# Two-layer masked attention on one core: putting the products with V off past large units of TensorE work

## The chip, the core and the metric

The kernel runs on one core of a Trainium2 chip. The metric is the device time of one execution in microseconds; the time before is the median of three runs.

## The reference

Two layers, each: layer norm with ReLU, masked multi-head attention with an adjacency mask, output projection, residual sum. There are 16 batches of 1024 rows with 256 features, all in float32. Layer 0 has 4 heads of 64 features, layer 1 has 8 heads of 32 and biases.

```python
# x (16, 1024, 256) float32, adj (16, 1024, 1024) int32, E = 256
def layer(x, adj, Wq, Wk, Wv, Wo, H, biases):
    h = maximum(layernorm(x), 0)
    q, k, v = heads(h, Wq), heads(h, Wk), heads(h, Wv)   # (16, H, 1024, E // H)
    s = einsum("bhnd,bhmd->bhnm", q, k) / sqrt(E // H)
    w = softmax(where(mask(adj), s, -inf), axis=-1)
    o = einsum("bhnm,bhmd->bhnd", w, v)
    return x + concat_heads(o) @ Wo.T + bo
x = layer(x, adj, ..., H=4)      # layer 0
x = layer(x, adj, ..., H=8)      # layer 1
```

## The kernel before

**Steps.** The attention is cut into *steps*. A step is four blocks of scores, each 128 keys by 512 queries, and everything that is done with them. Layer 0 of a batch has 16 steps (two heads and two key tiles each), layer 1 has 32 (four heads and one key tile each). The list of steps is fixed: layer 0 of batch 0, then, for each batch b, 16 steps of layer 0 of batch b+1 followed by 32 steps of layer 1 of batch b; the last batch leaves only the 32 of layer 1. In this document a+3 is the step with index 3 within such a block of 16, c+3 the step with index 3 within the block of 32 behind it. All blocks have an even number of steps, so a step's index is even or odd in the whole list as it is within its block. Groups of 4 (layer 0) or 8 (layer 1) steps share one accumulator `po`.

**What a step does.** `scores` (L364) multiplies K with Q on TensorE into two PSUM pairs `ps` (a pair is two banks; there are three pairs, L92, handed out in turn, and every other TensorE product except `po` and `pz` uses a pair of this same pool). `exponentials` has VectorE put the mask on each pair (L380, which frees the pair) and ScalarE take the exponential (L385), giving `p`. `weigh` (L396) multiplies `p` with V into `po`. `LEAD = 2`: step i of `Stream.run` issues the scores of step i and the products with V of step i-2.

**Column sums.** In layer 0 `add_tiles` adds blocks of `p` on VectorE and GpSimd (L407, L409). In layer 1 GpSimd adds the `p` of an odd step to that of the even step before it (L471), writing over the even one. `count` (L273) then multiplies with ones on TensorE into `pz`; it is entered in the list of things due two steps later. The tile `p` of even steps has three buffers, that of odd steps two.

**Units.** Between steps the other work of the stream is called from `self.due`, a table from step to calls that was filled by hand: `turn` (L195, transposes the normed rows), `k` and `q` (L207), `values` (L236) and, at the end of two groups, `end_half` (L345, output projection and residual). Each of `k`, `q`, `values` and `end_half` keeps TensorE busy for some 3.6 us; per batch there are 16 of them. Norm statistics (L160, L161), mask changes (L139), mask loads and transposes (L121, L125, L131) and the chain that inverts the sums (L288 to L316) hang on the same table.

**Shapes on TensorE.** Three kinds of product alternate, and the profile writes the part of the 128x128 array that each uses. Scores use row tiles, 64\*128 in layer 0 and 32\*128 in layer 1 (called R). `po` and `pz` use column tiles, 128\*64 and 128\*32 (called C). Units use the whole array, 128\*128 (called F). Order on each engine's queue is the order in which the program issues; no scheduler reorders.

**Start.** Before the stream the first batch's inputs and mask are made by straight code (L504 to L537): per tile of 128 rows, `load` (GpSimd's DMA queue), `flip` (a transposing DMA of SyncE's queue) and `put` (ScalarE, L131), with the first units among them.

Of the kernel before, what the change touches and what calls it, by code (L numbers as in the profile page):

```python
# [22 lines left out]
LEAD = 2  # L23
# [52 lines left out]
def fast_program(ctx, tc, a, w, loads, chk):  # L76
# [6 lines left out]
    NT = N // P  # L83
# [24 lines left out]
    def open_x(b, half):  # L108
        t = xp.tile([P, 4, E], F32, tag=f"x{half}", name=f"x_{b}_{half}")
        nc.sync.dma_start(t, x[b, ts(half, 512), :].rearrange("(t p) e -> p t e", p=P))  # L110
        xs[b, half] = t


    class Mask:
        def __init__(self, b):
            self.b, self.src, self.flipped = b, {}, {}
# [239 lines left out]
    def scores(st):  # L356
        gr = st.gr
        D = gr.D
        st.ps = [psum_pair(f"ps_{st.n}_{i}") for i in range(2)]
        st.blocks = []  # L360
        for i in range(4):
            r, kt = (i, st.j) if gr.layer else (i % 2, 2 * st.j + i // 2)
            st.blocks.append((r, kt))
            nc.tensor.matmul(  # L364
                st.ps[i // 2][:, i % 2, :],
                gr.inp.kT[r * D : (r + 1) * D, gr.g, ts(kt, P)],
                gr.inp.qT[r * D : (r + 1) * D, gr.g, ts(gr.qh, 512)],
                start=True, stop=True,
            )

    def exponentials(st, between):


        gr = st.gr
        odd = st.j % 2
        st.p = pp.tile([P, 4, 512], F32, tag=f"p{odd}", bufs=2 if odd else 3, name=f"p_{st.n}")
        for i in range(2):
            half = st.p[:, ts(i, 2), :]
            kt = st.blocks[2 * i][1]
            nc.vector.scalar_tensor_tensor(  # L380
                out=half,
                in0=gr.mask.m[:, kt, ts(gr.qh, 512)].unsqueeze(1).to_broadcast([P, 2, 512]),
                scalar=BIG, in1=st.ps[i], op0=ALU.mult, op1=ALU.min,
            )
            nc.scalar.activation(half, half, AF.Exp, scale=gr.scale)  # L385
            if i == 0:
                between()

    def weigh(st):
        gr = st.gr  # L390
        D = gr.D
        if st.j == 0:
            gr.o = ps_o.tile([P, 512], F32, tag="po", name=f"po_{gr.n}")
        for i, (r, kt) in enumerate(st.blocks):
            h = gr.g * gr.per + r
            nc.tensor.matmul(  # L396
                gr.o[r * D : (r + 1) * D, :], gr.inp.v[:, kt, h * D : (h + 1) * D],
                st.p[:, i, :], start=(kt == 0), stop=(kt == NT - 1),
            )

    def add_tiles(st):

        gr = st.gr
        t = work.tile([P, 2, 512], F32, tag="t", bufs=3, name=f"t_{st.n}")

        engine = nc.vector if st.j else nc.gpsimd
        engine.tensor_add(t, st.p[:, 0:2, :], st.p[:, 2:4, :])  # L407
        if st.j:
            nc.gpsimd.tensor_add(t, t, gr.t)  # L409
        gr.t = t  # L410

    def layer_steps(inp, mask):
        steps = []
        for qh in range(QH):
            half = Step()
            for g in range(2):
                steps += Group(inp, mask, qh, g, half).steps()
        return steps

    class Stream:  # L420

        def __init__(self, steps):
            self.steps, self.due = steps, {}

        def later(self, i, f, *args):
            self.due.setdefault(i, []).append((f, args))

        def run(self):  # L430
            steps = self.steps
            n = len(steps)
            for i in range(n + LEAD):
                now = steps[i] if i < n else None
                st = steps[i - LEAD] if i >= LEAD else None
                if now:
                    scores(now)
                copy = lambda: None
                if st:
                    weigh(st)  # L440
                    if st.gr.layer:
                        self.count_steps(i, st)
                    if st.last:
                        copy = st.gr.copy_out
                        self.end_group(i, st.gr)
                if now:
                    exponentials(now, copy)
                else:
                    copy()
                one = steps[i - 1] if 1 <= i <= n else None  # L450
                if one and one.gr.layer == 0:
                    add_tiles(one)
                for f, args in self.due.pop(i, []):
                    f(*args)
            while self.due:
                for f, args in self.due.pop(min(self.due)):
                    f(*args)
# [41 lines left out]
    def open_w(n):  # L499
        for _ in range(n):  # L500
            t, src = loads.pop(0)
            nc.sync.dma_start(t, src)

    masks = [Mask(b) for b in range(B)]  # L504
    inputs = [[Inputs(b, layer) for b in range(B)] for layer in range(2)]
    mask, inp = masks[0], inputs[0][0]
# [5 lines left out]
    inp.stats(0)  # L512
    inp.norm(0)
    inp.stats(1)
    inp.norm(1)
    for t in range(NT):
        mask.flip(t)
        mask.put(t)
        if t + 2 < NT:
            mask.load(t + 2)  # L520
        else:
            masks[1].load(t + 2 - NT)
        open_w(-(-len(loads) // 2))
        if t == 1:
            inp.turn(0)
            inp.k(0)
        if t == 3:
            inp.q(0)
            inp.turn(1)
        if t == 5:  # L530
            inp.values(0)
            inp.k(1)
    inp.q(1)
    inp.values(1)
    for half in range(QH):
        open_x(1, half)
        inp.add_bias(half)  # L537
# [14 lines left out]
    steps = layer_steps(inputs[0][0], masks[0])  # L552
# [11 lines left out]
    def norms(inp, half, i):  # L564

        later(i, inp.stats, half, (0, 1))
        later(i + 1, inp.stats, half, (2, 3))
        later(i + 3, inp.norm, half, (0, 1))
        later(i + 4, inp.norm, half, (2, 3))
        later(i + 5, inp.add_bias, half)  # L570

    def half_inputs(inp, half, *at):

        for i, f in zip(at, (inp.turn, inp.k, inp.q, inp.values)):
            later(i, f, half)
# [6 lines left out]
            later(2 * t + 1, masks[1].load, t + 2)  # L582
    for half in range(QH):
        norms(inputs[0][1], half, 3 * half)
    half_inputs(inputs[0][1], 0, 5, 6, 7, 8)
    half_inputs(inputs[0][1], 1, 9, 10, 11, 12)
    for b in range(B - 1):
        mine, a, c = inputs[1][b], first[b + 1], second[b]
        if b == 0:

            norms(mine, 0, a + 1)
            norms(mine, 1, a + 9)
            half_inputs(mine, 0, a + 6, a + 7, a + 8, a + 9)
            half_inputs(mine, 1, a + 15, c + 1, c + 4, c + 2)
        else:
            norms(mine, 0, a - 10)
            norms(mine, 1, a - 8)
            half_inputs(mine, 0, a - 4, a + 3, a + 4, a + 5)
            half_inputs(mine, 1, a - 2, a + 7, c + 4, c + 2)
        for kt in range(NT):  # L600
            later(a + 4 + kt, masks[b].second, kt)
        if b + 2 < B:
            other, mask = inputs[0][b + 2], masks[b + 2]
            later(a + 1, open_x, b + 2, 0)
            later(a + 11, open_x, b + 2, 1)
            norms(other, 0, a + 7)
            norms(other, 1, a + 15)
            half_inputs(other, 0, a + 14, c + 6, c + 10, c + 12)
            half_inputs(other, 1, c + 14, c + 16, c + 18, c + 20)
            for t in range(NT):  # L610
                i = a + 2 + 5 * t
                later(i, mask.load, t)
                later(i + 3, mask.flip, t)
                later(i + 5, mask.put, t)
        else:
            last = inputs[1][b + 1]
            norms(last, 0, c + 1)
            norms(last, 1, c + 9)
            half_inputs(last, 0, c + 6, c + 10, c + 12, c + 14)
            half_inputs(last, 1, c + 16, c + 20, c + 36, c + 34)  # L620
            for kt in range(NT):
                later(c + 8 + 2 * kt, masks[b + 1].second, kt)
# [162 lines left out]
def kernel(  # L785
# [28 lines left out]
    with ExitStack() as fast, tc.manual_schedule():  # L814
        fast_program(fast, tc, a, w, loads, chk)
# [61 lines left out]
```

## Time and profile before

| | |
|---|---|
| time, median of 3 runs | 3465.09 us (3464.63 to 3465.22) |
| profiled execution | 3465.88 us, its span 3464.0 us |
| granted TensorE clock | 0.997 |
| PE busy | 3402.7 us (98%), 18190 matmul rows |
| DVE busy | 2465.9 us (71%) |
| ACT busy | 2177.0 us (63%) |
| POOL busy | 2447.1 us (71%) |
| first scores on PE | 45.66 us |
| last matmul of the stream (L331) begins its group | 3446.98 us |

PE is TensorE, DVE VectorE, ACT ScalarE, POOL GpSimd, SP SyncE. A matmul of float32 is two rows of the profile. The end of a matmul row is modelled and overlaps with the next, so the busy share of PE says that it is seldom empty, not that it is streaming; the distance from the start of one group of rows to the start of the next is what a group really took.

### The profile page before, as it was taken

Reading aid. Unit: us, or ns where it says so; the run is one execution under the profiler, and the core shown is the slowest. Engines: PE = TensorE matmul, PEld = TensorE weight load, DVE = VectorE, ACT = ScalarE, POOL = GpSimd, SP = SyncE. Lnnn points to the kernel's source line nnn. Section 1 sums busy time; section 2 is a strip of 40 time slices with the busy share of each in tenths; the row PEclk is TensorE's granted clock in tenths of the full one; section 3 lists DMA queues with packets and bytes.
Section 4 is the critical chain, followed back from the end, with each engine's and each line's share of the span. In section 5 each row is a group of like instructions: output and inputs, shape, how many; then the busy total and the mean of one; then the engine's idle time right before and its main releaser. Section 6 shows DMA issues by size and latency. Waiting matters only on the chain. (4 is left out here: it accounts for less than half of the span.)

```text
span 3464.0 us, 46246 instructions
## 1 busy us (share of the span) xinstructions
PE 3402.7 (98%) x18190; PEld 1283.5 (37%) x18190; DVE 2465.9 (71%) x2664; ACT 2177.0 (63%) x2402; POOL 2447.1 (71%) x1606
## 2 busy tenths in 40 slices
PE   7999999999999999999999999999999999999998
PEld 3333333333333333333333433333333333333332
DVE  4777767777677676777767777677776776767776
ACT  5556566675666756667566675666756666665665
POOL 4677676776677766777667776677767777776766
PEclk9999999999999999999999999999999999999999
DMA  6121221211112121121211221212121121120000
GB/s 134 40 42 33 47 38 35 50 37 45 35 35 50 41 41 35 38 48 40 46 37 36 44 41 44 38 36 44 40 47 35 47 41 35 47 38 20 11 17 30
DMA packets 250738, 141.77 MB, mean 41 GB/s; under 512 B 182416, under 2 KB 217488, under 8 KB 250512
## 3 DMA queue, kind: packets, MB, share of 16 engines
q1 hardware_dynamic: 232080, 105.18, 12.6%
q0 software_dynamic: 18432, 33.56, 6.4%
q8 instruction: 144, 2.36, 0.3%
q14 instruction: 82, 0.67, 0.1%
HBM read 120.33 MB, written 18.34 MB: 40 GB/s over the span
## 5 line engine op out<-in xcount | busy, mean ns | idle before, releaser
L380 DVE SCALAR_TENSOR_TENSOR p<-mask,ps 128x1024 f32<-128x1024 fp8e4 x1536 | 1797.3, 1214 | 687.3 <-PE ps L364 682.5
L385 ACT ACTIVATE p<-p 128x1024 f32<-128x1024 f32 x1536 | 1613.4, 1056 | 1000.0 <-DVE p L380 959.2
L471 POOL TENSOR_TENSOR p<-p,p 128x2048 f32<-128x2048 f32 x255 | 1160.6, 4553 | 349.4 <-PE po L396 274.6
L364 PE MATMUL ps<-qT,kT 32*128 32x512 f32 (+1 forms) x6144 | 1172.0, 633 | 15.2 <-ACT hT L196 6.8
L396 PE MATMUL po<-p,v 128*32 128x512 f32 (+1 forms) x6144 | 1043.5, 606 | 14.8 <-ACT o L280 14.2
L409 POOL TENSOR_TENSOR t<-t,t 128x1024 f32<-128x1024 f32 x192 | 468.7, 2441 | 447.5 <-DVE t L407 415.6
L364 PEld LDWEIGHTS ps<-qT,kT 32*128 32x128 f32 (+1 forms) x6144 | 378.1, 184 | 722.3 <-issue 359.5
L396 PEld LDWEIGHTS po<-p,v 128*32 128x32 f32 (+1 forms) x6144 | 205.0, 117 | 749.5 <-issue 466.7
L407 DVE TENSOR_TENSOR t<-p 128x1024 f32<-128x1024 f32 x192 | 286.2, 1491 | 4.5 <-POOL t L409 4.5
L273 PE MATMUL pz<-p,ones 128*32 128x512 f32 x2056 | 267.7, 593 | 0.0
L207 PE MATMUL pq<-hT,wk 128*128 128x512 f32 x512 | 240.9, 614 | 8.1 <-ACT hT L196 8.1
L236 PE MATMUL pv<-wv,hT 128*128 128x256 f32 x1024 | 237.9, 385 | 0.0
L207 PE MATMUL pq<-hT,wq 128*128 128x512 f32 x512 | 236.6, 605 | 0.0
L345 PE MATMUL py<-wo,cat 128*128 128x256 f32 x1008 | 234.6, 386 | 0.5 <-POOL cat L316 0.5
L236 PEld LDWEIGHTS pv<-wv,hT 128*128 128x128 f32 x1024 | 189.4, 190 | 75.2 <-issue 28.9
L345 PEld LDWEIGHTS py<-wo,cat 128*128 128x128 f32 x1008 | 186.3, 190 | 75.3 <-issue 27.5
L316 POOL TENSOR_TENSOR cat<-o,inv 128x512 f32<-128x512 f32 x127 | 164.7, 1297 | 23.2 <-DMA inv<-vd 17.1
L407 POOL TENSOR_TENSOR t<-p 128x1024 f32<-128x1024 f32 x64 | 151.7, 2370 | 2.8 <-ACT p L385 2.4
L207 PEld LDWEIGHTS pq<-hT,wk 128*128 128x128 f32 x512 | 93.7, 193 | 154.9 <-issue 117.8
L131 ACT ACTIVATE mask<-adjT,mhalf 128x1024 fp8e4<-128x1024 bf16 x128 | 145.6, 1139 | 2.3 <-DMA adjT<-adj 2.1
L207 PEld LDWEIGHTS pq<-hT,wq 128*128 128x128 f32 x512 | 92.2, 189 | 144.3 <-issue 130.5
L177 ACT ACTIVATE hn<-x,shift,rstd 128x256 f32<-128x256 f32 x256 | 138.1, 587 | 11.0 <-POOL shift L170 11.0
(52 smaller groups left out, 1615.5 us busy)
## 6 DMA issues: line engine op xcount, KB each, us to landing
adj<-in_adj_dram POOLq DMA_DIRECT2D x128, 256.0 KB, 3.7
x<-in_x_dram SPq DMA_DIRECT2D x32, 512.0 KB
inv<-vd SPq DMA_DIRECT2D x128, 128.0 KB
inv<-vd SPq DMA_DIRECT2D x252, 64.0 KB
out_dram<-x SPq DMA_DIRECT2D x31, 512.0 KB
adjT<-adj SPq DMA_TRANSPOSE x128
sd<-s SPq DMA_DIRECT2D x64, 4.0 KB
sn<-sd SPq DMA_DIRECT2D x64, 4.0 KB
```

What stands on the lines that cost most here:

```text
L207: nc.tensor.matmul(pq[:, m, :], wt[self.layer][:, c, ts(m, P)], self.hT[half][:, c, :], start=(c == 0), stop=(c == 1),)
L236: nc.tensor.matmul(pv[:, i, :], self.hT[half][:, c, ts(i, P)], w.v[self.layer][:, c, :], start=(c == 0), stop=(c == 1),)
L273: nc.tensor.matmul(self.s[r * self.D : (r + 1) * self.D, :], w.ones[:, : self.D], p[:, r, :], start=start, stop=stop,)
L316: nc.gpsimd.tensor_mul(self.half.cat[:, self.g, :], self.ob, self.inv)
L345: nc.tensor.matmul(py[:, i, :], self.half.cat[:, c, ts(i, P)], w.o[self.layer][:, c, :], start=(c == 0), stop=(c == 1),)
L364: nc.tensor.matmul(st.ps[i // 2][:, i % 2, :], gr.inp.kT[r * D : (r + 1) * D, gr.g, ts(kt, P)], gr.inp.qT[r * D : (r + 1) * D, gr.g, ts(gr ...
L380: nc.vector.scalar_tensor_tensor(out=half, in0=gr.mask.m[:, kt, ts(gr.qh, 512)].unsqueeze(1).to_broadcast([P, 2, 512]), scalar=BIG, in1=st ...
L385: nc.scalar.activation(half, half, AF.Exp, scale=gr.scale)
L396: nc.tensor.matmul(gr.o[r * D : (r + 1) * D, :], gr.inp.v[:, kt, h * D : (h + 1) * D], st.p[:, i, :], start=(kt == 0), stop=(kt == NT - 1),)
L407: engine.tensor_add(t, st.p[:, 0:2, :], st.p[:, 2:4, :])
L409: nc.gpsimd.tensor_add(t, t, gr.t)
L471: nc.gpsimd.tensor_add(one, one, st.p)
```

## The change

`Stream.run` no longer calls `weigh` for step i-2 in every step i. Steps are put in a list `waiting`, and the list is emptied when i is odd or when nothing large (`k`, `q`, `values`, `end_half`) is due in step i. In an even step with something large due, `weigh` is left to step i+1, which calls it twice. What follows `weigh` (`count_steps`, `end_group`) is called with it. The table is altered so that large units stand at even steps: those called in layer 0's steps, and layer 0's own in the first 16. The inputs of the first batch are made in another order: the first `turn` goes ahead of the mask transposes, and the `put`s come later, in twos.

```diff
+        def large(self, i):
+            return any(
+                f.__name__ in ("k", "q", "values", "end_half") for f, _ in self.due.get(i, [])
+            )
@@ Stream.run
+            waiting = []
             for i in range(n + LEAD):
                 now = steps[i] if i < n else None
-                st = steps[i - LEAD] if i >= LEAD else None
+                if i >= LEAD:
+                    waiting.append(steps[i - LEAD])
                 if now:
                     scores(now)
                 copy = lambda: None
-                if st:
-                    weigh(st)
-                    if st.gr.layer:
-                        self.count_steps(i, st)
-                    if st.last:
-                        copy = st.gr.copy_out
-                        self.end_group(i, st.gr)
+                if i % 2 or not self.large(i):
+                    for st in waiting:
+                        weigh(st)
+                    for st in waiting:
+                        if st.gr.layer:
+                            self.count_steps(i, st)
+                        if st.last:
+                            copy = st.gr.copy_out
+                            self.end_group(i, st.gr)
+                    waiting = []
                 if now:
                     exponentials(now, copy)
@@ inputs of the first batch
     inp.stats(0)
     inp.norm(0)
     inp.stats(1)
-    inp.norm(1)
-    for t in range(NT):
-        mask.flip(t)
-        mask.put(t)
-        if t + 2 < NT:
-            mask.load(t + 2)
-        else:
-            masks[1].load(t + 2 - NT)
-        open_w(-(-len(loads) // 2))
-        if t == 1:
-            inp.turn(0)
-            inp.k(0)
-        if t == 3:
-            inp.q(0)
-            inp.turn(1)
-        if t == 5:
-            inp.values(0)
-            inp.k(1)
-    inp.q(1)
-    inp.values(1)
+    inp.turn(0)
+
+    def tiles(*ts):
+        for t in ts:
+            mask.flip(t)
+            (mask if t + 2 < NT else masks[1]).load((t + 2) % NT)
+            open_w(-(-len(loads) // 2))
+
+    tiles(0, 1)
+    inp.k(0)
+    inp.norm(1)
+    inp.q(0)
+    inp.turn(1)
+    mask.put(0)
+    mask.put(1)
+    inp.values(0)
+    tiles(2, 3)
+    inp.k(1)
+    mask.put(2)
+    mask.put(3)
+    tiles(4, 5)
+    inp.q(1)
+    mask.put(4)
+    mask.put(5)
+    tiles(6, 7)
+    inp.values(1)
+    mask.put(6)
+    mask.put(7)
@@ the table: half_inputs(inputs, half, turn, k, q, values)
-    half_inputs(inputs[0][1], 0, 5, 6, 7, 8)
-    half_inputs(inputs[0][1], 1, 9, 10, 11, 12)
+    half_inputs(inputs[0][1], 0, 5, 6, 8, 10)
+    half_inputs(inputs[0][1], 1, 11, 12, 14, 16)
@@ b == 0
-            half_inputs(mine, 0, a + 6, a + 7, a + 8, a + 9)
-            half_inputs(mine, 1, a + 15, c + 1, c + 4, c + 2)
+            half_inputs(mine, 0, a + 6, a + 8, a + 10, a + 12)
+            half_inputs(mine, 1, a + 15, c, c + 4, c + 2)
@@ b > 0
-            half_inputs(mine, 0, a - 4, a + 3, a + 4, a + 5)
-            half_inputs(mine, 1, a - 2, a + 7, c + 4, c + 2)
+            half_inputs(mine, 0, a - 4, a + 2, a + 4, a + 6)
+            half_inputs(mine, 1, a - 2, a + 8, c + 4, c + 2)
```

## The prediction

> **What bounds the kernel now.** I read the page's busy table first, then the table of who PE waited for, then PE's timeline.
>
> ```profile
> PE 3402.7 (98%) x18190; PEld 1283.5 (37%) x18190; DVE 2465.9 (71%) x2664; ACT 2177.0 (63%) x2402; POOL 2447.1 (71%) x1606
> PE po L396 <- ACT o L280: 14.2, 30, 0.7
> PE ps L364 <- DVE p L380: 6.3, 5, 2.6
> ```
>
> PE is the engine that sets the end: no other is over 71%, and its listed waits are few. But the ends of matmul rows are modelled, so real gaps hide inside the 98%. They show as distances between starts:
>
> ```profile
> 1290.19 1.14 PE L364 MATMUL ps<-qT,kT 32*128 32x512 f32 x8
> 1291.26 1.94 PE L396 MATMUL po<-p,v 128*64 128x512 f32 x8
> 1293.12 3.72 PE L345 MATMUL py<-wo,cat 128*128 128x256 f32 x16
> 1296.78 1.14 PE L364 MATMUL ps<-qT,kT 32*128 32x512 f32 x8
> 1297.85 1.94 PE L396 MATMUL po<-p,v 128*64 128x512 f32 x8
> 1299.71 1.79 PE L364 MATMUL ps<-qT,kT 32*128 32x512 f32 x8
> 1302.00 1.06 PE L396 MATMUL po<-p,v 128*32 128x512 f32 x8 [0.50 <-ACT o L280]
> ...
> 1307.65 1.14 PE L364 MATMUL ps<-qT,kT 32*128 32x512 f32 x8
> 1308.72 1.07 PE L396 MATMUL po<-p,v 128*32 128x512 f32 x8
> 1309.72 1.51 PE L364 MATMUL ps<-qT,kT 32*128 32x512 f32 x8
> 1311.16 1.06 PE L396 MATMUL po<-p,v 128*32 128x512 f32 x8
> 1312.16 3.70 PE L207 MATMUL pq<-hT,wq 128*128 128x512 f32 x8
> 1315.79 1.14 PE L364 MATMUL ps<-qT,kT 32*128 32x512 f32 x8
> 1316.86 1.07 PE L396 MATMUL po<-p,v 128*32 128x512 f32 x8
> 1317.74 1.04 PE L273 MATMUL pz<-p,ones 128*32 128x512 f32 x8
> 1318.71 1.14 PE L364 MATMUL ps<-qT,kT 32*128 32x512 f32 x8
> ```
>
> The second column is modelled, the first is when PE began. Within a group a new set of tiles starts each 0.427 us, so a layer-1 `po` streams 2 x 0.427 = 0.853 and a layer-0 `po` 1.707. Yet 1308.72 to 1309.72 is 0.996 and 1291.26 to 1293.12 is 1.868: each costs 0.143 or 0.161 more. Where `pz` follows `po` (both C), 1316.86 to 1317.74 is 0.883, and the 0.12 appears behind `pz`. Over all groups the medians are: R to C 0.21 over streaming, C to anything else 0.143 (32 columns) or 0.161 (64), F to R 0.22 to 0.24. So **a run of one kind costs some 0.11 at its end plus the first weight load at its start**.
>
> Beside this some steps are late: the scores at 1299.71 (step c+2) take 2.29 instead of 1.07. Summing such excess over the trace gives 121 us, nearly all in layer 1: c+2 16.1, c+4 5.6, c+23 to c+26 46.7, c+29 and c+31 22, c+15 6.7, c+10 and c+18 3.0.
>
> **What the Trainium skill says.** "TensorEngine Tiling", Key Properties: changing the tiling mode drains the engine. The trace agrees, with 0.11 where the kind changes and none between `po` and `pz`. "TensorE: Matmul & The Clock Gate", LDWEIGHTS: a load takes its columns over 1.2 ns, so 107, 53 and 27 ns for 128, 64 and 32 columns. With the 0.11 this gives 0.21, 0.16 and 0.14, the measured three. "SBUF — State Buffer", Who interferes with whom: VectorE in a two-port mode and GpSimd lock each other out. The trace has it: L139 takes 0.68 us, but 4.45 at 3290.10, ending as two GpSimd sums do. I use it below for the last batches only.
>
> **The change part by part.**
>
> 1. *Fewer runs.* Before, a large unit's surroundings are R C F R C; after, R F R CC. I counted runs in the instruction streams of both programs as built: 246 pairs of `po` now stand together (152 of layer 1, 94 of layer 0). Runs of C fall by 152 (32 columns) and by 78 (64 columns, since 16 `po` had been joined to a `pz` before), and two units now touch: 232 switches fewer of 1903. 152 x 0.143 + 78 x 0.161 + 2 x 0.22 = **34.7 us**, on PE's path. R to F does not occur in the trace before. I price it as R to C, 0.21, because the closing cost hardly depends on what follows. Without any drain it would save another 246 x 0.107 = 26; with a second load's worth on top it would cost 26.
>
> 2. *Steps c+0 to c+5.* At c+2 PE waits for a PSUM pair that VectorE has not read: VectorE is behind with statistics (1.08), the residual sum L350 (1.19) and sums (1.22). Moving `po` behind the next scores gives VectorE time. On the clock above, with VectorE's own durations: scores c+0 1290.19; L345 at 1291.26 to 1294.91; scores c+1 at 1294.91, their second pair held to 1295.9 as VectorE reads c+0 until 1295.80, so done by 1296.4; two `po` 1.76 + 1.82; scores c+2 1300.0 to 1301.07; then `values` needs the pair that VectorE frees at 1301.4, so 1301.5 to 1305.15; `pz`; scores c+3 at 1306.15, two `po`; c+4 at 1309.1, no wait; L207 1310.15; scores c+5 1313.8; c+6 at 1317.6 against 1318.71 before. That is 1.1 us a batch, 0.45 of it counted in 1: 15 x 0.65 = **9.8 us**. Two new waits (0.47 at c+1, 0.4 at c+2) eat half of what the old ones gave.
>
> 3. *Steps c+20 to c+27.* Here VectorE is the bound: exponentials' mask 2.35 plus statistics 1.1 in each step, from c+22 on. Scores of c+22 come 0.15 earlier, so VectorE's chain starts 0.17 earlier. At c+26 `po` also waited for ScalarE's copy of the last `po` (L280); it now goes to c+27, and L345 instead waits for the pair freed at about 1185.6 on that batch's clock (1187.29 before). Scores c+28 then come at 1193.1 against 1193.87: 0.8 a batch, 0.29 counted: 15 x 0.5 = **7.7 us**. At c+10 and c+18 the same copy is no longer waited for: **3.0 us**.
>
> 4. *Units moved to even steps* (k of a+3 to a+2, values a+5 to a+6, k a+7 to a+8, and in the first batches). No instruction is added; the copies to SBUF on ACT and DVE go along, and SP and POOL issue the same. Layer 0's steps have no PE waits before (2.6 us in all); for a pair of steps DVE has up to 10 us of work (masks 4.7, sums 2.4, q's copy 1.4, L139 1.4) in over 11 us of PE. Cost zero; a wait of 0.4 us in each of some 75 would be 30.
>
> 5. *GpSimd's sums L471* wait for the even step's `po`, which now comes a step later. In a pair with a unit that is 2.1 to 6.7 us after the pair's first scores, 4.55 more for the sum; `pz` reads it a pair (8.5 us) later. VectorE overwrites the odd `p` two steps later: margin 0.7 us at c+23, over 1 elsewhere. Cost zero.
>
> 6. *The start.* Now `turn` and `k` needn't wait for ScalarE's two `put`s (7.7 us on PE), but the last `put` still ends the chain: transposes wait for buffers freed by `put`, loads for the transposes (load 3.8, transpose 3.1 to 4 each). Step by step I get the first exponential at 47 to 50 us against 48.17 before. On POOL the bias sums (4.67) move back some 5 us. Zero, with -3 to +3.
>
> 7. *The last batches.* At c+20 and c+24 of batch 14 PE loses some 10 us to L139 locked out by GpSimd. Those sums move by up to 4 us; I take zero, -8 to +5.
>
> The sum is 34.7 + 9.8 + 7.7 + 3.0 = 55 us against the profiled execution's 3465.88 (span 3464.0, 1.9 around it): 3411. The median of the runs is 0.8 lower, which I leave inside the rounding: **3411 us**.
>
> **The rivals.**
>
> *R to F is dear.* A switch that is nowhere in the trace could cost 0.1 more: 26 us of the gain go, 3437. For it: row tiles and the whole array share all columns. Against: closing costs of 0.11 everywhere.
>
> *The waits come back elsewhere.* Items 2 and 3 rest on hand walks; if those waits only move, and GpSimd's margin of 0.7 fails (1 us in 15 batches), the gain is 35 - 15 = 20: 3446.
>
> *Slower: units starve for a PSUM pair.* A unit now follows its scores at once and takes the pair of the second half of the step before. In layer 1 that pair is read 3.5 us after those scores start, and the unit begins 4.85 after: margin 1.3 us, where before `po` gave 1.0 to 1.9 more. Were VectorE late by over 1.3 at most units, as it is at c+2 and c+26, each would lose 0.5: 246 x 0.5 = 123 less 35, 3553. It decides from 0.14 us a unit without items 2 and 3, 0.22 with them. Against it: VectorE idles 3.4 us ahead of most scores behind a unit.
>
> That the change does not do what it says is excluded by the built order.
>
> **How the numbers follow.** A measurement tells about 0.2%, 7 us, from no change. My forecast (gain 40 to 75) has 0.62, a dear switch or moved waits (gain 10 to 40) 0.22, a larger gain (cheap R to F, over 75) 0.04, no change 0.05, starving units 0.07. Faster 0.88, same 0.05, slower 0.07. The range, 3386 to 3446, takes in a free drain below, and the first two rivals above; it leaves out the slower one.
>
> **What would show it.** Right: L364 to L207 about 0.21 over streaming; pairs of `po` 0.85 apart; c+2 no longer at 2.3; no ACT o wait at PE. Wrong: units waiting for L380 of the step before at many steps, VectorE waiting for L471, or a start later than 3 us.

## The result and the profile after

| | before | after |
|---|---|---|
| median of 6 runs each | 3465.15 us (3464.13 to 3467.32) | 3404.89 us (3402.26 to 3405.98) |
| profiled execution, its span | 3465.88, 3464.0 us | 3402.26, 3400.5 us |
| granted TensorE clock | 0.997 | 0.996 |
| distance of one batch's block from the next, mean of batches 2 to 12 | 213.53 us | 209.41 us |

The ratio of after to before is **0.9825, 95% interval 0.9812 to 0.9838**: 60 us less, against 54 foretold (3411, range 3386 to 3446). The spans of the two profiled executions differ by 63.5 us; what follows from the traces is set against that.

The busy table and the table of whom PE waited for, of the kernel after. The second gives microseconds in all, times, and the longest:

```profile
PE 3359.3 (99%) x18190; PEld 1302.6 (38%) x18190; DVE 2468.8 (73%) x2664; ACT 2188.1 (64%) x2402; POOL 2446.0 (72%) x1606
```

```profile
PE py L345 <- DVE p L380: 2.5, 1, 2.5
...
PE po L396 <- ACT o L280: 0.5, 1, 0.5
```

These two tables tell little. The instructions are the same in number. Of the 30 waits for ScalarE's copy `o` one is left, which is 13.7 us less, and the 14 waits for its copy `hT` (6.8 us before) are gone; all rows of the second table together fall from 52.6 to 33.4 us. The other 44 us are in no row, because they lay behind the modelled ends of PE's rows. They show only as distances between starts. PE's timeline after, the same steps as those shown of before (the first row is step c+0), with start, duration, line, shape and count:

```profile
1274.07 1.14 PE L364 MATMUL ps<-qT,kT 32*128 32x512 f32 x8
1275.14 3.72 PE L345 MATMUL py<-wo,cat 128*128 128x256 f32 x16
1278.79 1.87 PE L364 MATMUL ps<-qT,kT 32*128 32x512 f32 x8
1280.59 3.65 PE L396 MATMUL po<-p,v 128*64 128x512 f32 x16
1284.17 1.14 PE L364 MATMUL ps<-qT,kT 32*128 32x512 f32 x8
1285.25 3.72 PE L236 MATMUL pv<-wv,hT 128*128 128x256 f32 x16
...
1298.60 1.92 PE L396 MATMUL po<-p,v 128*32 128x512 f32 x16
1300.34 1.04 PE L273 MATMUL pz<-p,ones 128*32 128x512 f32 x8
1301.32 1.14 PE L364 MATMUL ps<-qT,kT 32*128 32x512 f32 x8
```

- Two steps of `po` are one group of 16 rows. From 1298.60 to the `pz` at 1300.34 is 1.74 us, four tile sets of 0.427 and 0.03. The 64-column pair from 1280.59 to 1284.17 is 3.58, where two single ones at 1.868 made 3.74.
- Scores to a unit, the switch that before never had (R to F): 1284.17 to 1285.25, 1.08 us. The median over the trace is 1.071, or 0.218 over streaming. In layer 0 it is 0.211. **This is what R to C costs.**
- Step c+2 is no longer late: 1284.17 to 1285.25 instead of 2.29. Step c+1 is now the late one: 1278.79 to 1280.59 is 1.80, 0.73 too much, where 0.47 was foretold.

From c+0 (1274.07) to c+6 (1301.32) PE takes 27.25 us, against 28.52 in the lines shown of before.

**Where the time came from.** Distances between the starts of scores, a mean over batches 2 to 12, in us:

| steps | before | after | less |
|---|---|---|---|
| a+2 to a+12 | 58.91 | 58.30 | 0.61 |
| c+0 to c+6 | 28.53 | 27.25 | 1.28 |
| c+6 to c+10, c+12 to c+14, c+16 to c+18 | 34.52 | 33.99 | 0.53 |
| c+10 to c+12, c+18 to c+20 | 17.45 | 16.96 | 0.49 |
| c+20 to c+28 | 30.21 | 29.51 | 0.70 |
| c+28 to c+30 | 7.05 | 6.55 | 0.50 |
| the other steps | 36.86 | 36.85 | 0.01 |

This is 4.1 us a batch. The first and third rows are units where before had no wait: 0.13 or 0.14 for each of c+6, c+8, c+12 and c+16, the price of a run. The second, fourth and fifth rows hold both runs and waits; with the prediction's price for the runs in them (0.45, 0.28 and 0.29, not measured apart) switches make 0.61 + 0.53 + 1.02 = 2.16. The other 1.95 is waits. Over the whole trace, after is 4.5 us *behind* before at the fourth step and still 1.2 behind at the first layer-1 block's end; 13 equal batches bring 53.5; the block of batch 14 brings 10.8 instead of a usual 4.1.

### The profile page after: what moved, and what is told of

Its sections match the earlier page's. It is cut to its first block, busy times and chain, and to the rows that moved or that the text cites. A ratio compares the mean times of both kernels' runs of the same rounds, so it can differ in the third digit from the quotient of the medians.

```text
span 3400.5 us, 46245 instructions
## 1 busy us (share of the span) xinstructions
PE 3359.3 (99%) x18190; PEld 1302.6 (38%) x18190; DVE 2468.8 (73%) x2664; ACT 2188.1 (64%) x2402; POOL 2446.0 (72%) x1606
## 5 line engine op out<-in xcount | busy, mean ns | idle before, releaser
L380 DVE SCALAR_TENSOR_TENSOR p<-mask,ps 128x1024 f32<-128x1024 fp8e4 x1536 | 1801.3, 1215 | 753.7 <-PE ps L364 729.1
L482 POOL TENSOR_TENSOR p<-p,p 128x2048 f32<-128x2048 f32 x255 | 1163.0, 4562 | 399.9 <-PE po L396 396.1
L364 PE MATMUL ps<-qT,kT 32*128 32x512 f32 (+1 forms) x6144 | 1167.4, 633 | 13.1 <-DVE p L380 8.7
L396 PE MATMUL po<-p,v 128*32 128x512 f32 (+1 forms) x6144 | 989.9, 601 | 0.5 <-ACT o L280 0.5
L409 POOL TENSOR_TENSOR t<-t,t 128x1024 f32<-128x1024 f32 x192 | 479.1, 2495 | 401.3 <-DVE t L407 324.4
L364 PEld LDWEIGHTS ps<-qT,kT 32*128 32x128 f32 (+1 forms) x6144 | 375.0, 184 | 726.2 <-issue 364.0
L396 PEld LDWEIGHTS po<-p,v 128*32 128x32 f32 (+1 forms) x6144 | 229.1, 118 | 688.3 <-issue 529.3
L407 POOL TENSOR_TENSOR t<-p 128x1024 f32<-128x1024 f32 x64 | 171.5, 2680 | 0.4
```

Of the source, the lines that this page charges most:

```text
L364: nc.tensor.matmul(st.ps[i // 2][:, i % 2, :], gr.inp.kT[r * D : (r + 1) * D, gr.g, ts(kt, P)], gr.inp.qT[r * D : (r + 1) * D, gr.g, ts(gr ...
L380: nc.vector.scalar_tensor_tensor(out=half, in0=gr.mask.m[:, kt, ts(gr.qh, 512)].unsqueeze(1).to_broadcast([P, 2, 512]), scalar=BIG, in1=st ...
L396: nc.tensor.matmul(gr.o[r * D : (r + 1) * D, :], gr.inp.v[:, kt, h * D : (h + 1) * D], st.p[:, i, :], start=(kt == 0), stop=(kt == NT - 1),)
L482: nc.gpsimd.tensor_add(one, one, st.p)
```

## The experiments

A ratio refers to runs of before on the same chip. Step distances are means over batches 2 to 12, as in the table above.

**Table and start alone.** The loop weighs in every step, as before:

```diff
-                if i % 2 or not self.large(i):
+                if True:
```

> The changed kernel's table and start, but every step's products with V in their own step, as before. It has 1917 changes of the kind of product on TensorE, before has 1903. Theory (the gain is the runs saved by putting off, plus waits that only putting off removes): table and start alone bring nothing; the late start costs 4 to 5 us, so 3466 to 3472, and c+2 and c+26 still show scores of over 2 and 1.9 us. Rival (even placing of the units in the table relieves the engines): 3420 to 3445.

3470.0 us, ratio 1.0014 (1.0007 to 1.0021). The new places of the units and the new start bring nothing by themselves, in fact a loss of 2 to 7 us. A batch takes 213.69 us, and the late steps of before are all there (PE's timeline, step c+2 of the same batch, with its wait in brackets):

```profile
1304.90 1.78 PE L364 MATMUL ps<-qT,kT 32*128 32x512 f32 x8
1307.18 1.06 PE L396 MATMUL po<-p,v 128*32 128x512 f32 x8 [0.50 <-ACT o L280]
```

**Putting off alone**, with the table and the start of before:

```diff
-    half_inputs(inputs[0][1], 0, 5, 6, 8, 10)
+    half_inputs(inputs[0][1], 0, 5, 6, 7, 8)
...
-            half_inputs(mine, 0, a - 4, a + 2, a + 4, a + 6)
-            half_inputs(mine, 1, a - 2, a + 8, c + 4, c + 2)
+            half_inputs(mine, 0, a - 4, a + 3, a + 4, a + 5)
+            half_inputs(mine, 1, a - 2, a + 7, c + 4, c + 2)
```

> The table and the start of the kernel before, with the new loop that puts products with V off in even steps with a large unit. In layer 0 only a+4 and a+10 still qualify (3 units of 16 stand at odd steps). Theory: the gain of the change, less 3 x 0.16 x 15 = 7, plus the 4.5 us of the start that comes back: 3400 to 3412. Rival (the table is what counts): over 3430.

3410.43 us, ratio 0.9844 (0.9828 to 0.986). The loop alone brings 55 us. Only units in even steps put anything off, so 201 pairs of `po` form instead of 246: three units a batch stand in odd steps. Steps a+2 to a+12 take 58.61 us here, 58.91 before, 58.30 after.

**Putting off only where before had no wait.** At c+0, c+2, c+4, c+10, c+18, c+20 and c+26 the products are not put off:

```diff
-                if i % 2 or not self.large(i):
+                hold = i >= 16 and i < n - LEAD and (i - 16) % 48 - 16 in (0, 2, 4, 10, 18, 20, 26)
+                if i % 2 or hold or not self.large(i):
```

> The changed kernel, but products with V are not put off at c+0, c+2, c+4, c+10, c+18, c+20 and c+26, where the kernel before had waits on TensorE or close to them. Left are nine units a batch in steps that waited for nothing. Theory: only runs are saved there, 0.66 for layer 0's five and 4 x 0.143 for c+6, c+8, c+12 and c+16, 1.2 us a batch: 18 to 20 us less than the table alone, 3446 to 3453. Rival (the gain is all waits): the same as the table alone, 3466 to 3472.

3449.76 us, ratio 0.9955 (0.9938 to 0.9971), 20 us less than with the table alone. Its trace has 141 pairs, nine in a batch. Where they form, steps a+2 to a+12 take 58.30 us instead of 59.06 with the table alone, and those of the third row of the table above 33.97 instead of 34.53: 1.32 us for nine pairs, 0.147 each. So fewer runs are by themselves worth what a run costs. (That 141 times 0.143 makes 20.2, just the difference of the medians, is chance: each batch also gains 0.4 us in steps that were not put off, and this kernel is 3.7 us behind the table alone when the first layer-1 block ends.)

Putting off the other 105 pairs as well, which is after, brings 45 us more. A batch goes from 211.97 to 209.41 us, 2.56 less for seven more pairs, of which seven runs are 1.0. **The remaining 1.56 us a batch, 23 us in 15 batches, are waits that putting off removes.** The rest of the 45 us arises in the first and the last blocks of the list, where this experiment does not part runs from waits. Steps c+20 to c+28 take 30.21 us as before, and c+28 to c+30 take 7.06. That last one names a cause that I had not seen (PE's timeline of this kernel, the `pz` at the end of step c+29, then the scores of c+30):

```profile
1413.01 1.04 PE L273 MATMUL pz<-p,ones 128*32 128x512 f32 x8
1414.54 1.14 PE L364 MATMUL ps<-qT,kT 32*128 32x512 f32 x8 [0.49 <-ACT hT L196]
```

From 1413.01 to 1414.54 is 1.53 us, where 0.97 is usual: the scores wait for the pair that ScalarE's copy of the transposed rows (L196) has not freed. The waits of before list the same ("PE ps L364 <- ACT hT L196: 6.8, 14, 0.5"); those after do not list it. Which of the seven steps frees the pair in time was not tried.

**The scores of the odd step split** between the two `po`, which undoes the joining but leaves the later place:

```diff
+                split = bool(now) and len(waiting) == 2
...
-                    scores(now)
+                    scores(now, (0, 1) if split else range(4))
...
-                    for st in waiting:
+                    for k, st in enumerate(waiting):
+                        if k and split:
+                            scores(now, (2, 3))
                         weigh(st)
```

> The changed kernel, but where two products with V run in a row the second half of the step's scores is issued between them: the same matmuls in 246 x 2 more runs (R C R C in place of R CC). Theory (each run costs 0.11 at its end and its first weight load at its start): 246 x (0.107 + 0.107 + 0.14 to 0.16) = 89 us more than the changed kernel, 3485 to 3500. Rival (runs are free, waits were the gain): within 10 us of the changed kernel's 3405, or up to 25 more as the second half of the scores comes 0.9 to 1.8 us later.

3628.3 us, ratio 1.0477 (1.046 to 1.0495), far outside what I expected of either theory, because the edit changed more than the runs. PE's timeline of it: half the scores of a layer-0 step and its `po`, the same in layer 1, and a whole group of layer 1 (scores have line L365 here, `po` L397):

```profile
1311.90 1.13 PE L365 MATMUL ps<-qT,kT 64*128 64x512 f32 x4
1312.96 1.94 PE L397 MATMUL po<-p,v 128*64 128x512 f32 x8
...
1372.47 1.13 PE L365 MATMUL ps<-qT,kT 32*128 32x512 f32 x4
1373.53 1.06 PE L397 MATMUL po<-p,v 128*32 128x512 f32 x8
...
1377.44 1.14 PE L365 MATMUL ps<-qT,kT 32*128 32x512 f32 x8
1378.51 3.70 PE L207 MATMUL pq<-hT,wk 128*128 128x512 f32 x8
```

In layer 0 half the scores take 1.06 us, where a whole group takes 1.92. In layer 1 four rows take 1.06 us and eight take 1.07, because the eight fill four row tiles side by side and half of them fill two. So, by the price of a run, each split step of layer 1 paid 0.85 for a second group on top of the two runs, 0.33. Its trace has 492 runs more than after's, so 246 splits, 79 of them in layer 0 (next experiment): 167 x 1.18 + 79 x 0.36 = 225 us, against 223 measured. (The expectation of the next experiment speaks of 152 such steps of layer 1. That is the number of pairs of layer-1 `po`; 15 more pairs, of layer-0 `po`, stand behind scores of layer 1.)

**The same in layer 0 only**, where the halves are fair:

```diff
-                split = bool(now) and len(waiting) == 2
+                split = bool(now) and len(waiting) == 2 and now.gr.layer == 0
```

> As the split of the scores before, but only in layer 0's 79 steps with two products with V, where each half of the scores keeps its two row tiles side by side; in layer 1 a half of the scores used two of four row tiles and streamed as long as the whole, which adds 0.85 us to 152 steps and has nothing to do with runs. Theory: 158 runs more at 0.107 + 0.107 + 0.161 a pair, 79 x 0.35 to 0.38 = 28 to 30 us over the changed kernel: 3431 to 3437. Rival (runs are free): within 5 us of 3405.

3433.58 us (3432.04 to 3436.47), ratio 0.9912 (0.9896 to 0.9929). That is 28.7 us over after for 158 more runs, 0.18 each: one more run of C and one of R, 0.36 together, from unchanged work. Steps a+2 to a+12 take 60.06 us against 58.30, five splits of 0.35.

**The old start.** After, with the first batch's inputs made in the old order:

```diff
-    inp.turn(0)
...
-    tiles(0, 1)
-    inp.k(0)
     inp.norm(1)
-    inp.q(0)
...
+    for t in range(NT):
+        mask.flip(t)
+        mask.put(t)
...
```

> The changed kernel with the first batch's inputs in the old order. Theory A (the late start, 4.5 us at the fourth step, is lost for good): 3399 to 3402. Theory B (another chain, over batch 1's mask tiles and ScalarE, holds steps 6 to 8 anyway, as the run with x loaded early hints): the ninth step begins within 2 us of the changed kernel's 84.9 us, and the time is within 3 us of 3405.

3400.04 us (3399.71 to 3400.92), ratio 0.9813 (0.9797 to 0.983): 4.9 us less than after by the medians. The intervals of the two ratios overlap, but no run of one kernel reaches into the other's range, and the last experiment repeats the difference (5.6 us). **The new start costs some 2 to 6 us.** How it comes about is seen in after's timeline of the first 62 us (SPq is SyncE's DMA queue; PE's rows are the second half of the third step's scores, the `po` behind them, and the scores of the fourth and the ninth step):

```profile
45.85 1.15 SPq L110 DMA_DIRECT2D x<-in_x_dram  x2
48.74 1.99 ACT L385 ACTIVATE p<-p 128x1024 f32<-128x1024 f32 x2
51.96 0.43 DVE L160 BATCH_NORM_STATS2 st<-x 128x6 f32<-128x256 f32 x1 [7.21 <-DMA x<-in_x_dram]
54.29 2.08 PE L364 MATMUL ps<-qT,kT 64*128 64x512 f32 x4 [6.12 <-DVE p L380]
56.30 2.68 PE L396 MATMUL po<-p,v 128*64 128x512 f32 x8
58.90 1.99 PE L364 MATMUL ps<-qT,kT 64*128 64x512 f32 x8
...
84.92 1.99 PE L364 MATMUL ps<-qT,kT 64*128 64x512 f32 x8
```

The first exponential comes at 48.74 (48.17 before), inside the foretold 47 to 50. But the loads of batch 1's rows (L110) leave SP at 45.85 behind the mask transposes, 5.4 us later than before. VectorE stands 7.2 us at the statistics of these rows, and the masking of scores (L380) is queued behind. PE waits 6.1 us for the pair that L380 would free. In the trace the granted clock is 0.50 from 51.0 to 57.8 us: half the scores take 2.01 us (54.29 to 56.30) where 1.06 is usual, and the `po` 2.60 where 1.87 is usual, 1.7 us in all. The fourth step begins at 58.90, against 54.44 before and 53.53 with the old start.

Not all of this delay stays. With the old start PE's ninth step begins here:

```profile
82.72 1.99 PE L364 MATMUL ps<-qT,kT 64*128 64x512 f32 x8
```

So of the 5.4 us at the fourth step 2.2 are left at the ninth. These are kept: 2.2 us at the end of the first layer-1 block (354.23 against 352.04) and 2.3 at the last scores. The profiled execution of after is the fastest of its six, 2.6 us under their median; where the others lose more was not traced.

**Statistics earlier.** In after c+25 takes 4.18 us, 0.88 more than c+23 with the same products: VectorE has statistics in each step from c+22 on. They are put at c+16 to c+19, where VectorE has room:

```diff
-    def norms(inp, half, i):
+    def norms(inp, half, i, s=None):
...
-        later(i, inp.stats, half, (0, 1))
-        later(i + 1, inp.stats, half, (2, 3))
+        s = i if s is None else s
+        later(s, inp.stats, half, (0, 1))
+        later(s + 1, inp.stats, half, (2, 3))
...
-            norms(mine, 0, a - 10)
-            norms(mine, 1, a - 8)
+            norms(mine, 0, a - 10, a - 16)
+            norms(mine, 1, a - 8, a - 14)
```

> The changed kernel with the row statistics of layer 1's inputs (L160, L161, four stretches of 1.1 us on VectorE) moved from c+22 to c+25, where no large unit stands, to c+16 to c+19, where units leave VectorE idle; the norms stay where they are. Theory (VectorE is the bound from c+22 to c+26, because of these): c+24 falls from 2.47 to 2.07, c+25 from 4.18 to 3.30, c+26 from 5.20 to 4.70, 1.8 us a batch: 3374 to 3382. Rival (ScalarE or GpSimd bounds the stretch as well, at 2.1 and 2.3 us a step): 3395 to 3405.

3383.95 us (3382.54 to 3385.42), ratio 0.9765 (0.9748 to 0.9781): 21 us less than after, just short of the expected. PE's timeline, scores of c+24 and c+26; first after:

```profile
1163.22 1.55 PE L364 MATMUL ps<-qT,kT 32*128 32x512 f32 x8
...
1169.87 1.55 PE L364 MATMUL ps<-qT,kT 32*128 32x512 f32 x8
```

and then with the statistics earlier:

```profile
1160.71 1.14 PE L364 MATMUL ps<-qT,kT 32*128 32x512 f32 x8
...
1166.08 1.24 PE L364 MATMUL ps<-qT,kT 32*128 32x512 f32 x8
```

From c+24 to c+26 it is 5.37 us instead of 6.65, and step c+26 itself is 0.3 shorter.

**Statistics earlier in both places.** The statistics of layer 0's second half, with the norm and bias that follow them, also leave the steps around c+0:

```diff
-            norms(other, 1, a + 15)
+            norms(other, 1, a + 23)
```

> The one before, and the statistics of layer 0's second half with its norm and bias moved from a+15 (to c+4) to c+7 (to c+12). Theory (at c+1 the scores wait because VectorE reads the scores of c+0 late, behind these statistics): c+1 falls from 5.39 to about 4.7, 0.7 us a batch, so 8 to 11 us less than the one before, 3363 to 3374. Rival (VectorE is behind at c+0 for layer 0's column sums, not for the statistics): no less than 3 us below the one before.

3373.44 us, ratio 0.9735 (0.9718 to 0.9751), another 10.5 less. Step c+1, late in after by 0.73, is on time (PE's timeline: its scores and the pair of `po`, 1.07 us apart):

```profile
1270.32 1.14 PE L364 MATMUL ps<-qT,kT 32*128 32x512 f32 x8
1271.39 3.65 PE L396 MATMUL po<-p,v 128*64 128x512 f32 x16
```

**The same, with batch 1's rows loaded earlier:**

```diff
     tiles(2, 3)
+    open_x(1, 0)
+    open_x(1, 1)
...
-        open_x(1, half)
```

> The one before, and batch 1's rows loaded on SyncE's queue ahead of the last four mask transposes instead of behind them. Theory (the late start comes from VectorE, whose statistics of batch 1 wait 7.2 us for these rows with the masks of the next scores queued behind): the fourth step begins some 4 us earlier, 3 to 6 us less than the one before. Rival (the start is set by the chain of mask tiles, which these loads delay): no less, or up to 3 us more.

3374.22 us (3371.75 to 3376.62), ratio 0.9736 (0.9719 to 0.9752): no gain where 3 to 6 us were expected. The first half of the chain did what I said: the fourth step begins at 54.54 us instead of 59.52. But the ninth begins at 87.82, later than the 85.71 without this edit, with new waits of 1.3 and 2.2 us for L380 between. The mask transposes stand behind the row loads now, and what hangs on them is late in its turn. So the late load is what delays the fourth step, but moving that load alone wins nothing at the end. An order of the new start that does was not tried.

**Both, with the old start:**

```diff
+            norms(mine, 0, a - 10, a - 16)
+            norms(mine, 1, a - 8, a - 14)
...
+            norms(other, 1, a + 23)
```

> The version with both statistics moved, with the old order of the first inputs. Theory A: 4 us less than its 3373.4, 3368 to 3371. Theory B: within 3 us of it.

**3367.87 us** (3367.63 to 3368.69), ratio 0.9721 (0.9705 to 0.9737), the best of all: 97 us under before and 37 under after.

## Why the prediction was right, and where its steps were off

Gains over the trace in us (a loss is negative), foretold and measured. Measured are the distances of the table above, times 15 as in the prediction (14 for c+29), with the runs split off as said there, so that 15.3 of the 32.4 us are the prediction's own price. After's trace is 1.2 us behind before's at the end of the first layer-1 block, where an equal batch would have put it 4.1 ahead: 5.3 us are missing, 2.2 of them by the start (what the trace with the old start has less), the others with either start. The last batches are what batch 14 brings beyond 4.1:

| step of the prediction | foretold | measured |
|---|---|---|
| 1, fewer runs | 34.7 | 32.4 |
| 2, c+0 to c+5 beyond runs | 9.8 | 12.5 |
| 3, c+20 to c+27 beyond runs | 7.7 | 6.2 |
| 3, c+10 and c+18 | 3.0 | 3.2 |
| c+29, in no step | none | 7.0 |
| 6, the start | 0 (-3 to 3) | -2.2 (by medians -4.9) |
| the first 64 steps otherwise, in no step | none | -3.1 |
| 7, the last batches | 0 (-5 to 8) | 6.7 |
| sum | 55 | 63 |

1. **Fewer runs** was right in kind and size. 246 pairs are there, R to F costs 0.21 as priced, and the first rival, a dear R to F, is gone. The Trainium skill ("TensorEngine Tiling", Key Properties) says that a change of tiling mode drains the engine; here a run of layer 0 costs 0.18 us (28.7 us for 158 runs), drain and first load together. How it divides between the two is not shown: the trace's own weight loads take 0.19, 0.14 and 0.11 us for 128, 64 and 32 columns, each some 0.08 more than the figures that the prediction added to its 0.11, and only their differences agree.
2. **Steps c+0 to c+5** gave 1.28 a batch for 1.1. The two new waits were one: 0.73 at c+1, none at c+2. The walk had the right engine, VectorE, but not the right step: freeing the statistics from there (10.5 us) shows that it is these that make c+1 late.
3. **Steps c+20 to c+27** gave 0.70 for 0.8. That VectorE's chain is what holds PE there was right: the earlier statistics take 1.6 us a batch from it.
4. **Units in even steps** at no cost was nearly right: the table under the old loop adds 0.16 us a batch. Under the new one, with the same start, it is worth 10 us (3410.4 to 3400.0): 0.3 us a batch for its 45 more pairs, 4.4 us that are there by the first layer-1 block's end, and 1.8 in the block of batch 14. One stretch does pay: layer 0 of batch 1 takes 92.0 us after, 87.6 before, and 87.3 with before's table under the new loop. What is late there was not looked into.
5. **GpSimd's sums** cost PE nothing, as I said, but the place that I named was wrong, and a wait that I had called a sign of being wrong is there. The margin did not fail at c+23. It fails at a+1, once a batch, where VectorE waits before it may overwrite `p` (GpSimd's sum is L471 before and L482 after; after's waits, and one place of its timeline):

```profile
DVE p L380 <- POOL p L482: 22.9, 15, 1.6
```

```profile
1197.03 2.35 DVE L380 SCALAR_TENSOR_TENSOR p<-mask,ps 128x1024 f32<-128x1024 fp8e4 x2 [1.59 <-POOL p L482]
```

   Steps a+0 and a+1 take 6.69 us in both kernels, so VectorE's 1.6 us are hidden there.

6. **The start** failed. The fourth step begins 4.5 us later than before, beyond the 3 that I had allowed, and the term of 0 should have been between -2 and -5. I followed the chain to the first exponential, which came when I said, and stopped there. The loads of the *next* batch's rows stand on SP's queue behind the transposes, and VectorE reaches their statistics ahead of the masks of step 3. I had looked at what moved on POOL's queue, and had not asked what SP's held up.
7. **The last batches** went to the good end of the range, 6.7 for a term of 0. VectorE's mask change (L139) against GpSimd's sum, at c+23 of batch 14, after:

```profile
3249.22 4.57 POOL L482 TENSOR_TENSOR p<-p,p 128x2048 f32<-128x2048 f32 x1 [10.54 <-PE po L396]
...
3254.11 0.69 DVE L139 TENSOR_SCALAR mask<-mask 128x1024 fp8e4<-128x1024 fp8e4 x1
```

   and with the table alone:

```profile
3316.22 4.55 POOL L482 TENSOR_TENSOR p<-p,p 128x2048 f32<-128x2048 f32 x1 [3.87 <-PE po L396]
3317.35 3.97 DVE L139 TENSOR_SCALAR mask<-mask 128x1024 fp8e4<-128x1024 fp8e4 x1
```

   The later `po` moved GpSimd's sums, and here L139 falls just behind one instead of into it: 0.69 us, not 3.97. The lockout is what the Trainium skill ("SBUF — State Buffer", Who interferes with whom) describes: the two engines share a pair of ports, and the one that comes second waits for the other's whole instruction. Step c+24 of that batch fell from 7.08 us to 2.07. The step had the mechanism and the place; its sign would have needed the times of all three engines worked out. No run moves L139 by itself, so that the place of the sum is the cause is read from these two traces, not tried.

   The lockout is not all of it; the step had no term for the clock. At c+20 L139 is locked out before, after and in the best kernel alike (4.4 us), and PE then waits 2.55 to 2.6 us for the scores' second pair. Behind this wait the granted clock drops in some executions and not in others. After, then the kernel with both statistics moved and the old start (PE's timeline, and a stretch of it with the engines' busy times; the third number from the end is the granted clock):

```profile
3240.42 1.13 PE L364 MATMUL ps<-qT,kT 32*128 32x512 f32 x4 [2.55 <-DVE p L380]
3241.55 5.40 PE L207 MATMUL pq<-hT,wk 128*128 128x512 f32 x8
3242.47:3245.88 3.41, 3.41 (x5) 1.33 (x4) 1.89 (x3) 2.49 (x4) 0.00 (x0) 0.50 0.03 6
```

```profile
3206.03 1.13 PE L364 MATMUL ps<-qT,kT 32*128 32x512 f32 x4 [2.55 <-DVE p L380]
3207.16 3.70 PE L207 MATMUL pq<-hT,wk 128*128 128x512 f32 x8
3206.03:3210.79 4.76, 4.76 (x12) 1.74 (x13) 3.94 (x4) 4.46 (x5) 0.00 (x0) 1.00 0.01 3
```

   The same lockout and the same wait give a step of 10.14 us with 3.4 us at half clock and of 8.44 without. Before has two such stretches in this block, 6.8 us each from 3295.8 and from 3316.3, behind the waits of c+20 and c+24. From the distances between starts I estimate that they cost 6.1 us, and the one after 1.7. So some 4.4 of the 6.7 us are PE at full clock again, and the lockout that is gone at c+24 makes up the rest. That the waits bring the lower clock on is read from their order, not tried.

The wait at c+29 was in a row of the waits of before that I did not quote or price, though my own sum of late steps had 22 us at c+29 and c+31. It and the last batches (13.7 together) outweigh the start and the first steps (-5.3), which is why the gain was above 55. The large terms were right by their mechanism. That the four which were missing or put at nothing, 13.7 and -5.3, leave the sum only 8 us off is luck. The rival of waits that only move is refuted by the 23 us of the 105 pairs. The slower one, units that starve for a PSUM pair, came true at c+26 alone: from the scores to the unit it is 0.48 us more there than elsewhere, 6.7 us in 14 batches, a wait that step 3 had counted. PE's list of waits shows none of this, only one unit that waits 2.5 us for L380 once.

## What to carry to other kernels

Where shapes of different kinds alternate on TensorE, count the runs and price a run from start-to-start distances: joining two saved 0.13 to 0.15 us here wherever nothing else was waiting, and the busy share (98%, then 99%) showed neither the runs nor the late steps. Putting work off behind a long unit also gives the other engines time, and half of the gain here was that; ask of each unit which engine was late beside it. When a start is reordered, follow every queue to the second consumer, not only to the first result. And look at the granted clock behind each long wait of PE before a late stretch is put down to the wait alone.

## What the hardware showed that I had not expected

Half of a layer-1 group of scores (two row tiles of 32 instead of four) takes 1.06 us, the whole 1.07: with two tiles filled the set takes as long as with four. And a wait of PE of 2.5 us can cost more than its length: behind it the granted clock was 0.50 for 3.4 us in one execution, and the unit that followed took 5.33 us; in another, behind the same wait, it stayed at 1.00 and the unit took 3.63.
